# A selective-scan recurrence on one core: delta*u moved from GpSimd to VectorE, two products with C per batch moved the other way, softplus and the first inputs rearranged

## The chip, the core and the metric

The kernel runs on one core of one Trainium2 chip. The metric is the device time of one launch in microseconds (us). A profiled execution of the same program gives a trace: each instruction with its engine, its start, its duration and, where the engine stood idle ahead of it, what released it. The engines are TensorE (PE), VectorE (DVE), ScalarE (ACT), GpSimd (POOL) and SyncE (SP), which issues most DMAs. Each works through its own queue in order.

## What is computed

The whole program is a state-space layer, a mixture of experts with 64 experts, a cross attention and a quantised feed-forward layer over x of 4 x 512 x 512. The change lies in the first part alone. Cut to that, for each batch:

```python
x  = einsum('ed,bld->bel', in_proj_w, ctx)          # 512 channels, 512 steps
u  = silu(depthwise_conv(x, conv_w) + conv_b)
dt_lo, Bm, Cm = split(einsum('ke,bel->bkl', x_proj_w, u), [16, 16, 16])
delta = softplus(einsum('er,brl->bel', dt_proj_w, dt_lo) + dt_proj_b)
def step(state, d_t, B_t, C_t, u_t):                # state: channels x 16
    state = state * exp(d_t * A) + (d_t * u_t) * B_t
    return state, (state * C_t).sum(-1)
y = (scan(step) + D * u) * silu(layernorm(x_in))
x_out = x_in + y
```

## The kernel before

The channels lie on the 128 partitions in NC = 4 chunks c, and the 512 time steps in the free dimension. For a batch b (of 4) and a chunk c, the 16 states are taken two at a time, so that a pair of states is one tile of 128 x 1024. That makes 8 pairs i per chunk, 32 per batch, and a list `seq` of 128 steps q = (b, c, i) that one Python loop (L676) writes out. The loop's order of calls is the order of each engine's queue: the section runs under a manual schedule, and nothing reorders it. I call the eight steps of one (b, c) a **block**, and s = q % 32 the step within the batch.

What one step q does:

- `inputs(q + 2)` (L494), POOL: dBu = B (from `bb`, rows broadcast to all partitions) times du (delta*u), 128 x 1024, into one of three buffers. It runs two steps ahead; its buffer is that of step q - 1, which that step's scan must have read.
- `decays(q + 1)` (L502), ACT: two exponentials of delta into a dA tile in PSUM, of which there are two, so that step q - 1 must be done with its own. At s = 22 and s = 28 the decays of steps 24 and 30 are made early instead, in SBUF (`early=True`, L506).
- `scan(q)` (L513), DVE: the scan over dA and dBu (L524). Then the product with C (L525). For i in 0, 2 and 4 the scan writes to SBUF (`hc`) and POOL takes the product; for the others the scan writes in place over dA, and DVE takes the product.
- `sums(q - 1)` (L534), PE: eight transposes onto one PSUM tile `yT` sum the states; `result` (L562) multiplies the finished tile by the gate on DVE at i = 2 of the next block.

Once per block, for the block after: at i = 2 a matmul makes `pdt` in PSUM (L425); at i = 3 ACT runs `steps_a` and `steps_ln` (L428 to L443: e = |pdt|, relu = max(pdt, 0), e = exp(-e), pdt = 1 + e, ln); at i = 4 DVE runs the three instructions of `steps_b` (L450 to L452), which add max(pdt, 0) and ln(1 + e) with a correction; at i = 5 POOL makes du = delta*u (L460) and writes the reset value into delta's first column (L463). The tiles `pdt` lie in PSUM; `e`, `ln`, `delta`, `u` and `du` lie in SBUF.

Meanwhile the queues carry the next batch's projection, convolution and activations (`ahead`, `ahead_ends`), and the values and keys of the later attention on PE, ACT and SP. In `ahead`, at s = 26 `norm` (L384) makes 1/std on POOL with a power and -mean/std, at s = 29 `silu_gz` (L394) uses both on ACT, and at s = 26, 28 and 30 `rows` loads B and C by DMA.

Ahead of the loop (L648 to L674) the first batch is prepared: convolution, `tables` (an ACT table load, L242), project, softplus, `step_du`, and the inputs of steps 0 and 1.

Of the kernel before, what the change touches and what calls it, by code (L numbers as in the profile page):

```python
# [17 lines left out]
F32 = mybir.dt.float32  # L18
# [6 lines left out]
AF = mybir.ActivationFunctionType  # L25
ALU = mybir.AluOpType
# [4 lines left out]
P = 128  # L31
B, S, DM = 4, 512, 512
NT = B * S // P
NC = DM // P
CTX = 256
EPS = 1e-5
# [32 lines left out]
RESET = 1e30  # L69
# [172 lines left out]
def tables(nc):  # L242

    nc.scalar.preload_act_table_set("natural_log_exp_and_others")
# [3 lines left out]
def ssm_phase(ctx, cm, x_all, w, kv, router_stats):  # L248
# [4 lines left out]
    tc, nc = cm.tc, cm.nc  # L253
    pool = {n: ctx.enter_context(tc.tile_pool(name=f"a_p{n}", bufs=n)) for n in (1, 2, 3, 4, 5)}
# [15 lines left out]
    st = {}  # L270
# [17 lines left out]
    for n, shape in (("conv_w", [P, NC, DC]), ("conv_b", [P, NC]), ("D", [P, NC])):  # L288
        t = vecs[n] = cp.tile(shape, F32, name=f"v_{n}")
# [78 lines left out]

    def silu_0(c):
        nc.scalar.activation(st[0]["u"][c], st[0]["u"][c], AF.Silu)  # L370
        if c == NC - 1:
            tables(nc)

    def silu_u(b):
        for u in st[b]["u"]:
# [8 lines left out]
    def norm(b):  # L384
        s = st[b]
        ve = small.tile([P, NC], F32, name="ve_a")
        nc.gpsimd.tensor_scalar(ve, s["mv"][:, :, 1], EPS, None, ALU.add)
        s["rstd"] = small.tile([P, NC], F32, name="rstd_a")
        nc.gpsimd.tensor_tensor(s["rstd"], ve, half, ALU.pow)
        s["nmr"] = small.tile([P, NC], F32, name="nmr")  # L390
        nc.gpsimd.tensor_tensor(s["nmr"], s["mv"][:, :, 0], s["rstd"], ALU.mult)
        nc.gpsimd.tensor_scalar(s["nmr"], s["nmr"], -1.0, None, ALU.mult)

    def silu_gz(b):  # L394
        s = st[b]
# [7 lines left out]
    def project(b):  # L403
        pd = st[b]["pd"] = ps.tile([R, S], F32, name="pd", tag="pa")
        for c in range(NC):
            nc.tensor.matmul(pd, xpT[:, c, :], st[b]["u"][c], start=c == 0, stop=c == NC - 1)

    def take_project(b):

        xd = st[b]["xd"] = pool[1].tile([R, S], F32, name="xd")  # L410
        nc.scalar.activation(xd, st[b]["pd"], AF.Identity, bias=cm.ident[0:R, DR:DR + 1])
        nc.sync.dma_start(bc_dram[b], xd[R // 2:, :])

    def rows(b, g):

        for name, row in (("bb", g * NG), ("cb", DS + g * NG)):
            t = pool[4].tile([P, NG, S], F32, name=name, tag=name)
            nc.sync.dma_start(
                t, bc_dram[b, row:row + NG, :].unsqueeze(0).to_broadcast([P, NG, S]))
            st[b][name].append(t)  # L420
# [7 lines left out]
    def steps_a(b):  # L428

        s = st[b]  # L430
        pdt = s["pdt"]
        s["e"] = pool[1].tile([P, S], F32, name="e")
        s["relu"] = pool[2].tile([P, S], F32, name="delta")
        nc.scalar.activation(s["e"], pdt, AF.Abs)
        nc.scalar.activation(s["relu"], pdt, AF.Relu)
        nc.scalar.activation(s["e"], s["e"], AF.Exp, scale=-1.0)

    def steps_ln(b):

        s = st[b]  # L440
        nc.scalar.activation(s["pdt"], s["e"], AF.Identity, bias=cm.ones[:, 0:1])
        s["ln"] = pool[1].tile([P, S], F32, name="ln", tag="yg")
        nc.scalar.activation(s["ln"], s["pdt"], AF.Ln)  # L443

    def steps_b(b):


        s = st[b]
        t, delta = s.pop("pdt"), s.pop("relu")
        nc.vector.scalar_tensor_tensor(t, t, 1.0, s["e"], ALU.subtract, ALU.subtract)  # L450
        nc.vector.tensor_tensor(t, s["ln"], t, ALU.subtract)
        nc.vector.tensor_tensor(delta, delta, t, ALU.add)  # L452
        s["delta"].append(delta)

    def step_du(b):
        s = st[b]
        c = len(s["du"])
        delta = s["delta"][c]
        du = pool[2].tile([P, S], F32, name="du")
        nc.gpsimd.tensor_tensor(du, delta, s["u"][c], ALU.mult)  # L460


        nc.gpsimd.memset(delta[:, 0:1], RESET)  # L463
        s["du"].append(du)


# [17 lines left out]
    def take_values(b, n):  # L484
        g, kc = divmod(n, S // P)
        v = pool[2].tile([P, HG * HD], F32, name="v")
        nc.scalar.copy(v, pvs.pop((b, n)))
        nc.sync.dma_start(kv["v"][b, g, :, kc, :], v)
# [2 lines left out]
    seq = [(b, c, i) for b in range(B) for c in range(NC) for i in range(NP)]  # L491
    dBus, dAs, hcs, yTs = {}, {}, {}, {}

    def inputs(q):  # L494
        if q < len(seq):
            b, c, i = seq[q]
            j = i % 2 * 2
            dBus[q] = pool[3].tile([P, 2, S], F32, name="dBu")
            nc.gpsimd.tensor_tensor(dBus[q], st[b]["bb"][i // 2][:, j:j + 2, :],  # L499
                                    st[b]["du"][c].unsqueeze(1).to_broadcast([P, 2, S]), ALU.mult)  # L500

    def decays(q, early=False):  # L502

        if q < len(seq) and q not in dAs:
            b, c, i = seq[q]
            dAs[q] = (pool[2].tile([P, 2, S], F32, name="dA") if early else  # L506
                      pda.tile([P, 2, S], F32, name="dA"))
            for j in range(2):
                n = 2 * i + j
                nc.scalar.activation(dAs[q][:, j, :], st[b]["delta"][c], AF.Exp,  # L510
                                     scale=negA[:, c, n:n + 1])

    def scan(q):  # L513


        b, c, i = seq[q]
        j = i % 2 * 2
        cb = st[b]["cb"][i // 2][:, j:j + 2, :]
        hc = hcs[q] = pool[3].tile([P, 2, S], F32, name="hc")
        dA, dBu = dAs.pop(q), dBus.pop(q)  # L520
        on_pool = i in (0, 2, 4)
        h = hc if on_pool else dA
        flat = [t.rearrange("p a s -> p (a s)") for t in (h, dA, dBu)]
        nc.vector.tensor_tensor_scan(*flat, 0.0, ALU.mult, ALU.add)  # L524
        (nc.gpsimd if on_pool else nc.vector).tensor_tensor(hc, h, cb, ALU.mult)  # L525
# [20 lines left out]
    def direct(b, c):  # L546
        st[b]["Du"] = pool[1].tile([P, S], F32, name="Du")
        nc.scalar.activation(st[b]["Du"], st[b]["u"][c], AF.Copy, scale=vecs["D"][:, c:c + 1])
# [13 lines left out]
    def result(b, c):  # L562
        xv = x_all[:, b * NC:(b + 1) * NC, c * P:(c + 1) * P]
        if b + 1 < B:
            nc.vector.tensor_tensor(xv, yTs.pop((b, c)), st[b]["gzT"], ALU.mult)  # L565
            if c == NC - 1:
                nc.gpsimd.dma_start(x_all[:, b * NC:(b + 1) * NC, :],
                                    w["x"][b * S:(b + 1) * S, :].rearrange("(c p) d -> p c d", p=P),
                                    accum_op=ALU.add)
            return  # L570
        t = pool[1].tile([P, NC, P], F32, name="yg")
        nc.vector.tensor_tensor(t, yTs.pop((b, c)), st[b]["gzT"], ALU.mult)
        nc.gpsimd.tensor_tensor(xv, xv, t, ALU.add)
# [69 lines left out]
    def key_steps(q, ends):  # L643
        for f, a in key_plan.pop((q, ends), ()):
            f(*a)
# [11 lines left out]
    silu_0(3)  # L657
    project(0)
    take_project(0)
    rows(0, 0)  # L660
    for c in range(NC):
        stats(0, c)
# [5 lines left out]
    step_du(0)  # L668
    decays(0)
    decays(1)  # L670
    inputs(0)
    inputs(1)
    load_wv(0)
    for g in range(1, DS // NG):  # L674
        rows(0, g)
    for q, (b, c, i) in enumerate(seq):  # L676
        inputs(q + 2)

        ahead_of = b + 1 < B and q % 2 == 0 and q > 0
        if ahead_of:  # L680
            take_values(*last)
        decays(q + 1)
        key_steps(q, False)
        if b > 0 and q % SL == 1:
            rows(b, DS // NG - 1)
        if i == 2 and q > 2:
            result(*seq[q - 3][:2])
        scan(q)
        if i == 1:
            direct(b, c)  # L690
        if q == 0:
            silu_gz(0)
        if q % SL == 8 and b + 1 < B:
            load_x(b + 1)
        if i == 2:
            take_gate(b, c)

        to = seq[q // NP * NP + NP][0:2] if q + NP < len(seq) else None
        if to is not None:
            if i == 3:  # L700
                steps_a(to[0])
                steps_ln(to[0])
            if i == 5:
                step_du(to[0])
        if b + 1 < B:
            ahead(b + 1, q % SL)
        if i == 1:
            gate(b, c)
        if q % 8 == 2 and q + 8 < len(seq):
            load_wv(q // 2 + 4)  # L710
        if q % 2:
            values((b + 1) % B, q % SL // 2, wvs[q // 8])
        elif q > 0 and not ahead_of:
            take_values(*last)
        last = (b + 1) % B, q % SL // 2
        sums(q - 1)
        if to is not None:
            if i == 2:
                dt(*to)
            if i == 4:  # L720
                steps_b(to[0])
        if b + 1 < B:
            ahead_ends(b + 1, q % SL)
        key_steps(q, True)
# [1876 lines left out]
```

## Time and profile before

| what | value |
|---|---|
| median of 3 timed runs | 2467.73 us (2467.22 to 2468.25) |
| the profiled execution's own time | 2456.93 us |
| its span, first to last instruction | 2455.2 us |
| granted TensorE clock, mean | 0.982 |
| first scan starts, last scan starts | 34.46 us, 503.07 us |
| scans (L524) | 128 of 2300 or 2347 ns mean by form |
| products with C (L525) | 80 on DVE of 1256 ns, 48 on POOL of 2412 ns |
| inputs dBu (L499) | 128 on POOL of 2411 ns |
| delta*u (L460) | 16 on POOL of 1731 ns (1261 to 3277) |
| softplus on DVE (L450, L451, L452) | 16 each of 685, 696 and 686 ns |
| Relu on ACT (L435) | 16 of 596 ns |

The page's first part gives each engine's busy time; another view gives busy time by stretch; the timeline lists the instructions of one engine, with start, duration, engine, line, output<-inputs, shape and count, and in brackets the idle time ahead of them and what ended it. Two instructions of one engine may overlap by a tenth of a microsecond in it.

From the starts of the scans in the timeline, the time from the first scan of a block to the first scan of the next, in us:

| batch | c = 0 | c = 1 | c = 2 | c = 3 |
|---|---|---|---|---|
| 0 | 28.92 | 28.14 | 29.89 | 33.55 |
| 1 | 28.00 | 28.14 | 29.49 | 33.57 |
| 2 | 28.13 | 28.13 | 29.50 | 33.56 |
| 3 | 31.06 | 27.78 | 27.79 | 25.39 (to the last product) |

### The profile page before, as it was taken

The numbers are of one execution on the slowest core, as the hardware profiler recorded it, in microseconds if no ns is written. First come the engines' busy times: TensorE is split into PE (matmuls) and PEld (weight loads), VectorE is DVE, ScalarE is ACT, GpSimd is POOL, SyncE is SP. The second block draws the span as 40 slices with busy tenths as digits, with TensorE's granted clock in tenths as the row PEclk, the third lists the DMA queues.
The fourth block names the chain that finished last, engine by engine and source line by source line (L and its number), as shares of the span: only waits on it lengthen the run. The fifth ranks groups of instructions, "written<-read, shape, count | busy, mean of one in ns | idle before, by whom it ended". The sixth has DMA issues, their size and how long they took to land. (4 is left out here: it accounts for less than half of the span.)

```text
span 2455.2 us, 29177 instructions
## 1 busy us (share of the span) xinstructions
PE 2324.5 (95%) x8819; PEld 1264.5 (52%) x8819; DVE 1587.6 (65%) x2872; ACT 1413.3 (58%) x2647; POOL 1329.0 (54%) x1314
## 2 busy tenths in 40 slices
PE   6999899988999999999998899999999999999998
PEld 2555555655555656667674444444444444444444
DVE  6999998966244434444334577667776777666655
ACT  6777777755323333344433466666666676667654
POOL 7999999950444434544444356356644564333323
PEclk8999998999999999999999999999999999999999
DMA  5363727343789878899996488678867887676630
GB/s 214 91 230 95 237 88 247 112 152 122 213 262 289 266 227 275 274 284 341 297 275 205 147 197 208 152 183 208 191 149 168 181 200 170 137 155 148 135 75 26
DMA packets 479891, 468.01 MB, mean 191 GB/s; under 512 B 313247, under 2 KB 354287, under 8 KB 475632
## 3 DMA queue, kind: packets, MB, share of 16 engines
q1 hardware_dynamic: 433390, 303.41, 46.7%
q0 software_dynamic: 42992, 160.13, 20.7%
q10 hardware_dynamic: 3346, 2.54, 0.3%
q8 instruction: 72, 1.18, 0.2%
q14 instruction: 91, 0.75, 0.1%
HBM read 316.11 MB, written 79.82 MB: 161 GB/s over the span
## 5 line engine op out<-in xcount | busy, mean ns | idle before, releaser
L1350 PE MATMUL pg<-xT,wg 128*128 128x284 f32 (+12 forms) x1536 | 390.6, 400 | 3.5 <-ACT xT L1337 2.1
L2086 POOL COPY planes<-e 128x512 int16<-128x512 int16 x174 | 118.8, 683 | 397.6 <-DVE e L2067 227.7
L2058 DVE TENSOR_REDUCE mx<-psc 128x1 f32<-128x512 f32 x256 | 176.1, 688 | 239.7 <-PE psc L2055 239.0
L1350 PEld LDWEIGHTS pg<-xT,wg 128*128 128x128 f32 x1536 | 281.2, 192 | 94.4 <-issue 39.1
L499 POOL TENSOR_TENSOR dBu<-bb,du 128x1024 f32<-128x1024 f32 x128 | 304.7, 2411 | 6.1 <-DVE dA L524 5.3
L2061 ACT ACTIVATE e<-psc,mx 128x512 f32<-128x512 f32 x256 | 176.1, 688 | 152.6 <-DVE mx L2058 82.2
L2055 PE MATMUL psc<-kT,qT 128*128 128x512 f32 x512 | 260.1, 594 | 0.7 <-ACT qT L2049 0.7
L2127 PE MATMUL po<-eT,v 128*128 128x512 f32 x512 | 236.8, 605 | 13.7 <-ACT eT L2121 11.9
L1271 POOL DMA_INDIRECT xg<-xn_dram,tok x168 | 176.0, 1047 | 120.0 <-PE pt L1314 58.3
L2021 PE MATMUL pq<-Wq,xnT 128*128 128x512 f32 x512 | 232.1, 596 | 3.9 <-ACT xnT L1977 3.6
L2136 PE MATMUL px<-Wo,oT 128*128 128x512 f32 x512 | 231.2, 595 | 2.3 <-DVE qn L2039 2.3
L510 ACT ACTIVATE dA<-delta,negA 128x512 f32<-128x512 f32 x256 | 176.4, 694 | 53.0 <-DVE hc L525 38.6
L524 DVE TENSOR_TENSOR_SCAN dA<-dA,dBu 128x1024 f32<-128x1024 f32 x80 | 184.0, 2300 | 17.6 <-ACT dA L510 11.1
L1271 POOL DMA_INDIRECT wd<-down,widx x64 | 61.6, 962 | 228.7 <-PE po L1384 219.4
L2127 PEld LDWEIGHTS po<-eT,v 128*128 128x128 f32 x512 | 92.0, 189 | 151.1 <-issue 91.8
L2021 PEld LDWEIGHTS pq<-Wq,xnT 128*128 128x128 f32 x512 | 96.1, 191 | 127.6 <-issue 108.9
L2136 PEld LDWEIGHTS px<-Wo,oT 128*128 128x128 f32 x512 | 95.1, 190 | 125.4 <-issue 105.8
L530 PEld LDWEIGHTS yT<-ident,hc 128*128 128x128 f32 x1024 | 118.7, 143 | 73.4 <-issue 45.3
L1395 ACT COPY yo<-po 128x512 f32<-128x512 f32 (+3 forms) x64 | 37.4, 585 | 193.8 <-PE po L1384 147.7
L530 PE MATMUL yT<-ident,hc 128*128 128x128 f32 x1024 | 132.0, 276 | 16.6 <-DVE x_all L565 10.2
L1395 DVE COPY yo<-po 128x512 f32<-128x512 f32 x68 | 46.9, 690 | 150.2 <-PE po L1384 150.2
L2067 DVE TENSOR_SCALAR e<-e,tot 128x512 f32<-128x512 f32 x256 | 129.0, 504 | 13.5
(380 smaller groups left out, 4671.7 us busy)
## 6 DMA issues: line engine op xcount, KB each, us to landing
y_dram<-yo SPq DMA_DIRECT2D x110, 256.0 KB
bb<-bc_dram SPq DMA_DIRECT2D x16, 1024.0 KB
cb<-bc_dram SPq DMA_DIRECT2D x16, 1024.0 KB
v_dram<-v SPq DMA_DIRECT2D x64, 256.0 KB
kT<-k_dram SPq DMA_DIRECT2D x64, 256.0 KB
rk<-r_dram SPq DMA_DIRECT2D x64, 256.0 KB
v<-v_dram SPq DMA_DIRECT2D x64, 256.0 KB
Wo<-Wo SPq DMA_DIRECT2D x60, 256.0 KB
```

Source lines behind the costliest of these rows:

```text
L499: nc.gpsimd.tensor_tensor(dBus[q], st[b]["bb"][i // 2][:, j:j + 2, :], st[b]["du"][c].unsqueeze(1).to_broadcast([P, 2, S]), ALU.mult)
L510: nc.scalar.activation(dAs[q][:, j, :], st[b]["delta"][c], AF.Exp, scale=negA[:, c, n:n + 1])
L524: nc.vector.tensor_tensor_scan(*flat, 0.0, ALU.mult, ALU.add)
L530: nc.tensor.matmul(yT[:, lc, :], t[:, lc * P:(lc + 1) * P], cm.ident, is_transpose=True, start=first and lc == 0, stop=last, skip_group_ch ...
L1271: nc.gpsimd.indirect_dma_start(out=t[0:n, :], out_offset=None, in_=table, in_offset=bass.IndirectOffsetOnAxis(ap=index, axis=0))
L1350: nc.tensor.matmul(pg[:, 0:n], s["wg"][:, c, m * P:(m + 1) * P], s["xT"][:, c, 0:n], start=c == 0, stop=c == NC - 1)
L2021: nc.tensor.matmul(pq.rearrange("p h d -> p (h d)"), xnTs[b * NC + i][:, c, :], s["Wq"][:, c, :], start=c == 0, stop=c == NC - 1)
L2055: nc.tensor.matmul(pscore, st[b, g]["qT"][:, h, i * P:(i + 1) * P], ks[n], start=True, stop=True)
L2058: nc.vector.tensor_reduce(mx, pscore, AX.X, ALU.max, negate=True)
L2061: nc.scalar.activation(e, pscore, AF.Exp, bias=mx, accum_out=tot)
L2127: nc.tensor.matmul(po, v[:, kc, :], eT[:, kc, :], start=kc == 0, stop=kc == KB - 1)
L2136: nc.tensor.matmul(px, oTs[j * HG + h][:, i * P:(i + 1) * P], st[b, g]["Wo"][:, h, :], start=h == 0, stop=h == HG - 1)
```

## The change

1. `step_du`: the product delta*u and the write of the reset value go from POOL to DVE, and are called at i = 4 right behind `steps_b`, not at i = 5.
2. `scan`: the product with C of i = 6 goes from DVE to POOL for c = 1 and c = 2 of all batches but the last (six products); that of the very first step goes from POOL to DVE.
3. Softplus: ACT no longer makes the Relu; 1 + e goes to a tile `near` in SBUF (the later delta) and not over `pdt` in PSUM; the correction is worked out in that SBUF tile; the last DVE instruction reads `pdt` from PSUM, takes its maximum with 0 and adds.
4. `norm`: the addition of epsilon goes from POOL to DVE, and the two small instructions that make -mean/std become one on DVE. The power stays on POOL between them.
5. The inputs of step 0 are made by DVE.
6. At the start, the second ACT table load comes behind `take_project(0)`, not ahead of `project(0)`.

```diff
     def silu_0(c):
         nc.scalar.activation(st[0]["u"][c], st[0]["u"][c], AF.Silu)
-        if c == NC - 1:
-            tables(nc)
...
         ve = small.tile([P, NC], F32, name="ve_a")
-        nc.gpsimd.tensor_scalar(ve, s["mv"][:, :, 1], EPS, None, ALU.add)
+        nc.vector.tensor_scalar(ve, s["mv"][:, :, 1], EPS, None, ALU.add)
         s["rstd"] = small.tile([P, NC], F32, name="rstd_a")
         nc.gpsimd.tensor_tensor(s["rstd"], ve, half, ALU.pow)
         s["nmr"] = small.tile([P, NC], F32, name="nmr")
-        nc.gpsimd.tensor_tensor(s["nmr"], s["mv"][:, :, 0], s["rstd"], ALU.mult)
-        nc.gpsimd.tensor_scalar(s["nmr"], s["nmr"], -1.0, None, ALU.mult)
+        nc.vector.scalar_tensor_tensor(s["nmr"], s["mv"][:, :, 0], -1.0, s["rstd"], ALU.mult,
+                                       ALU.mult)
...
-        s["relu"] = pool[2].tile([P, S], F32, name="delta")
+        s["near"] = pool[2].tile([P, S], F32, name="delta")
         nc.scalar.activation(s["e"], pdt, AF.Abs)
-        nc.scalar.activation(s["relu"], pdt, AF.Relu)
         nc.scalar.activation(s["e"], s["e"], AF.Exp, scale=-1.0)
...
-        nc.scalar.activation(s["pdt"], s["e"], AF.Identity, bias=cm.ones[:, 0:1])
+        nc.scalar.activation(s["near"], s["e"], AF.Identity, bias=cm.ones[:, 0:1])
         s["ln"] = pool[1].tile([P, S], F32, name="ln", tag="yg")
-        nc.scalar.activation(s["ln"], s["pdt"], AF.Ln)
+        nc.scalar.activation(s["ln"], s["near"], AF.Ln)
...
-        t, delta = s.pop("pdt"), s.pop("relu")
-        nc.vector.scalar_tensor_tensor(t, t, 1.0, s["e"], ALU.subtract, ALU.subtract)
-        nc.vector.tensor_tensor(t, s["ln"], t, ALU.subtract)
-        nc.vector.tensor_tensor(delta, delta, t, ALU.add)
+        pdt, delta = s.pop("pdt"), s.pop("near")
+        nc.vector.scalar_tensor_tensor(delta, delta, 1.0, s["e"], ALU.subtract, ALU.subtract)
+        nc.vector.tensor_tensor(delta, s["ln"], delta, ALU.subtract)
+        nc.vector.scalar_tensor_tensor(delta, pdt, 0.0, delta, ALU.max, ALU.add)
...
-        nc.gpsimd.tensor_tensor(du, delta, s["u"][c], ALU.mult)
+        nc.vector.tensor_tensor(du, delta, s["u"][c], ALU.mult)
...
-        nc.gpsimd.memset(delta[:, 0:1], RESET)
+        nc.vector.memset(delta[:, 0:1], RESET)
...
-    def inputs(q):
+    def inputs(q, by=nc.gpsimd):
...
-            nc.gpsimd.tensor_tensor(dBus[q], st[b]["bb"][i // 2][:, j:j + 2, :],
+            by.tensor_tensor(dBus[q], st[b]["bb"][i // 2][:, j:j + 2, :],
                                     st[b]["du"][c].unsqueeze(1).to_broadcast([P, 2, S]), ALU.mult)
...
-        on_pool = i in (0, 2, 4)
+        on_pool = q > 0 and (i in (0, 2, 4) or i == 6 and c in (1, 2) and b + 1 < B)
...
     take_project(0)
+    tables(nc)
...
-    inputs(0)
+    inputs(0, nc.vector)
...
-            if i == 5:
-                step_du(to[0])
...
             if i == 4:
                 steps_b(to[0])
+                step_du(to[0])
```

## The prediction

> **What bounds the kernel now.** I read the page's first part, then busy time by stretch, then who waits for whom from 30 to 510 us, then the timelines of VectorE and GpSimd over batch 1. The first view is one batch of the recurrence:
>
> ```profile
> 155.00:275.00 120.00, 109.90 (x482) 64.89 (x483) 111.92 (x82) 89.18 (x146) 114.18 (x58) 0.96 0.50 163
> ```
>
> Of 120 us PE is busy 109.9, DVE 111.9, ACT 89.2 and POOL 114.2. So no single engine has room to take work for nothing, and only DVE's queue is in every step. DVE's waits, from 30 to 510 us (total, times, longest):
>
> ```profile
> DVE dA L524 <- ACT dA L510: 11.1, 9, 2.0
> DVE dA L524 <- POOL dBu L499: 4.5, 5, 1.6
> DVE pdt L450 <- ACT ln L443: 4.2, 3, 2.5
> DVE hc L524 <- POOL dBu L499: 3.9, 1, 3.9
> ```
>
> DVE stands for some 30 us out of 475 in all, and only 8.4 of them are put down to POOL, 3.9 of those at the start. The recurrence is therefore paced by DVE's own instructions. From the timeline's starts, a scan with POOL's product costs DVE 2.2 us, a scan with its own product 3.52, a result 0.6 and softplus this much:
>
> ```profile
> 167.79 2.28 DVE L524 TENSOR_TENSOR_SCAN hc<-dA,dBu 128x1024 f32<-128x1024 f32 x1
> 169.98 0.67 DVE L450 SCALAR_TENSOR_TENSOR pdt<-pdt,e 128x512 f32<-128x512 f32 x1
> 170.69 0.70 DVE L451 TENSOR_TENSOR pdt<-ln,pdt 128x512 f32<-128x512 f32 x1
> 171.42 0.69 DVE L452 TENSOR_TENSOR delta<-delta,pdt 128x512 f32<-128x512 f32 x1
> 172.03 2.29 DVE L524 TENSOR_TENSOR_SCAN dA<-dA,dBu 128x1024 f32<-128x1024 f32 x1
> ```
>
> The scan of i = 4 ends at 170.07 and the next starts at 172.03: 1.96 us. A block's floor is 3 x 2.2 + 5 x 3.52 + 0.6 + 2.05 = 26.85 us; blocks c = 0 to 2 take 28.0 to 29.9 with their statistics (0.81 each). What follows the recurrence needs all of its x, so I pass its time on one to one.
>
> **The row that decides.** Nearly every DVE instruction in the loop has one input in PSUM and at most one in SBUF. The exceptions are steps 24 and 30 of a batch, whose dA lies in SBUF. DVE, then POOL, around both in batch 1:
>
> ```profile
> 240.59 3.34 DVE L524 TENSOR_TENSOR_SCAN hc<-dA,dBu 128x1024 f32<-128x1024 f32 x1
> ...
> 264.32 2.69 DVE L524 TENSOR_TENSOR_SCAN dA<-dA,dBu 128x1024 f32<-128x1024 f32 x1
> 267.11 2.05 DVE L525 TENSOR_TENSOR hc<-dA,cb 128x1024 f32<-128x1024 f32 x1
> ```
>
> ```profile
> 239.43 2.37 POOL L499 TENSOR_TENSOR dBu<-bb,du 128x1024 f32<-128x1024 f32 x1 [1.11 <-DVE dA L524]
> ...
> 262.51 2.35 POOL L499 TENSOR_TENSOR dBu<-bb,du 128x1024 f32<-128x1024 f32 x1
> 264.83 3.26 POOL L460 TENSOR_TENSOR du<-delta,u 128x512 f32<-128x512 f32 x1
> 268.14 0.10 POOL L463 MEMSET delta<- 128x1 f32 x1
> 268.24 7.76 POOL L499 TENSOR_TENSOR dBu<-bb,du 128x1024 f32<-128x1024 f32 x3
> ```
>
> The scan of 3.34 is 1.06 over the usual 2.28: it works only from about 241.65, as POOL's dBu ends (241.80). The scan at 264.32 gains 0.4, to the end of POOL's dBu at 264.86. POOL's du, 1.28 at its median, then takes 3.26, as if begun at 266.8 when that scan ends. DVE's product at 267.11, 1.23 as a rule, ends at 269.16: begun at 267.93, as du ends. And POOL's three dBu, 6.99 elsewhere, take 0.77 more. So an instruction of DVE with two inputs in SBUF and one of POOL that reads SBUF take turns, each whole, and **the one that was waiting goes next**, even between two DVE instructions that follow on one another. The handover comes some 0.15 to 0.2 ahead of the recorded end. At 1410.59 a DVE instruction with two SBUF inputs (L1950, median 746 ns) takes 2.06 and ends 0.56 after POOL's product of 1410.82 to 1412.09. DMA does not explain it:
>
> ```profile
> 240.00:244.00 4.00, 4.00 (x22) 2.46 (x21) 4.00 (x3) 3.96 (x8) 1.79 (x1) 1.00 0.17 66
> 264.00:268.00 4.00, 4.00 (x16) 2.64 (x15) 3.90 (x3) 3.97 (x6) 4.00 (x2) 0.59 1.01 410
> ```
>
> The DMA engines are full in the second stretch but at 0.17 in the first, with the larger delay.
>
> The page "SBUF — State Buffer" of the Trainium skill, section "Who interferes with whom", says the same against this change: a VectorE instruction with two SBUF inputs and a GpSimd one that reads SBUF hold a shared port pair in turn, each for its whole length. Taken to the letter a turn costs 2.35 and not the 2.0 I use below; over two turns in each of 15 blocks that would be some 10 us more.
>
> **Part by part.**
> *Softplus and du (parts 1 and 3).* Today none of L450 to L452 has two SBUF inputs. After the change the first (near, e), the second (ln, near) and du (delta, u) do; the third reads PSUM. I take their lengths from L450 to L452, 0.65 to 0.7. POOL is free of du and waits at the product of i = 4 when that scan ends at T (its dBu was made before); DVE's first instruction starts at T - 0.09 and goes first, to T + 0.6. POOL's product then runs, 2.35, and holds the second one back by 2.0: T + 2.6 to 3.3. POOL's next dBu takes the turn (3.1 to 5.45), the third DVE instruction hides beside it, du waits to 5.3 and ends at 5.95. The scan of i = 5 starts at T + 5.95, today at T + 1.96: **+4.0 us a block**, du's own 0.65 included. The memset (0.06) is lost in it. Below, 2.0 a block if only one turn is lost; above, 6.2 if POOL is in mid-instruction at T and the first one waits a whole 2.2 as well.
> *Products to POOL (part 2).* DVE saves 3.52 - 2.2 = 1.32 in c = 1 and c = 2 of three batches; POOL, with time to spare now, hides 2.33.
> *Waits that go.* The small stalls at i = 2 and i = 6 come from PE and ACT running late, and those get time: I take 0.6 in c = 0, 0.3 in c = 1, 0.5 in c = 2. So c = 0: 4.0 - 0.6 = +3.4; c = 1: 4.0 - 1.32 - 0.3 = +2.4; c = 2: +2.2.
> *Norm (part 4), a new wait.* DVE's second instruction of s = 26 now needs POOL's power, which stands behind POOL's product of that step:
>
> ```profile
> 251.20 2.35 POOL L525 TENSOR_TENSOR hc<-hc,cb 128x1024 f32<-128x1024 f32 x1 [0.19 <-DVE hc L524]
> ...
> 253.96 1.04 POOL L389 TENSOR_TENSOR rstd_a<-ve_a,half 128x4 f32<-128x4 f32 x1
> ...
> 255.57 4.66 POOL L499 TENSOR_TENSOR dBu<-bb,du 128x1024 f32<-128x1024 f32 x2
> ```
>
> The scan of s = 26 ends at 251.06, the product at 253.55, the power about 1.05 later at 254.6. The next dBu starts at once and DVE's instruction, with two SBUF inputs, waits for it: ready at about 256.9. Queued behind it on DVE is the scan of s = 27, which starts at 250.97 today: 5.9 later (3.6 without the turn). Then 3.52, a scan of 2.2 and softplus at 5.95 put the scan of s = 29 at 268.6. Today it starts at 260.78 after 1.97 us of waiting for ACT; that wait, and the 1.45 at s = 31 behind `silu_gz`, are swallowed. Carried on (3.52, 1.0 for a turn at scan 30, then 3.5), s = 31 starts at 276.6 against 270.61: **+6.0 for c = 3**.
> *Last batch.* Its stall on ACT ln shrinks by the Relu's 0.48, but POOL's product is then already under way, so three full turns give T + 7.05; today the scan of i = 5 starts T + 4.68 (c = 0) and T + 2.95 (c = 1, c = 2): 2.4 + 4.1 + 4.1 = +10.6. Block c = 3 has no softplus.
> *Start (parts 5 and 6).* ACT's Relu (0.48) and POOL's du against DVE's (1.26 - 0.65) come off the way to the first decays: 1.1 to 1.5. The input by DVE may have to take turns with POOL's second input, 2.3 at worst, but scan 2 waits for ACT and the second B rows (37.6) anyway. I take -1.5. The moved table load gains 0.15.
>
> **Sum.** 3 x (3.4 + 2.4 + 2.2 + 6.0) + 10.6 - 1.5 = 42 + 10.6 - 1.5 = **+51, say 50 us**. The profiled execution's own time, 2456.93 with a span of 2455.2, would become 2507. The timed runs have a median 10.8 above it; with the same 50 they come to **2518 us**. Its own range is 2483 to 2552: below, one turn a block and no turn at norm (next paragraph, less 3 x 2.3); above, 15 x 2.2 more.
>
> **Rivals.** *One turn a block* (0.18): DVE keeps its place between dependent instructions, and only du waits: +2.0 a block, c = 0 to 2 then +1.4, +0.4, +0.2, c = 3 +4.0, last batch +6: 3 x 6 + 6 - 1.5 = +22, 2490. Against it stands the product at 267.11, which had to wait though it followed its scan.
> *No turns* (0.09): the long instructions have another cause. Then du costs 0.65, the products give 1.32 back, the norm wait of 3.6 goes into the waits of 1.97 and 1.45 behind it: about 3 x (0.65 - 0.7 - 0.7) + 0.6 - 1.5 = -3, 2465. The stretch at 240 speaks against it.
> *GpSimd paces the loop* (0.07), the faster case: POOL is the busiest, 114.2 of 120, and gives up 16 du and memsets (27.7 + 1.6), three small instructions a batch (2.6), one product and one input (4.7), and takes six products (14): -22.6, 2445. It decides if POOL never stands and DVE mostly waits for it; but only 8.4 of DVE's 30 us of waiting are for POOL.
>
> **Chances.** Forecast 0.66, one turn 0.18, no turns 0.09, GpSimd 0.07. About 0.2% (5 us) is what a measurement of this kernel can tell from no change: slower 0.84, within 0.09, faster 0.07. The range 2483 to 2552 leaves out the last two, 0.16.
>
> **What would show it.** In the new profile the second softplus instruction and du on DVE last 2 us and more, ending just after POOL's products or dBu, while the third stays at 0.7; the scan of i = 5 starts some 6 us after that of i = 4 ends; at s = 27 DVE idles 3.5 us for POOL's power; POOL's idle time grows and its busy share in the loop falls. If these three DVE instructions last 0.7, the turns were wrong and so is the forecast; if DVE's waits for POOL vanish with a shorter block, GpSimd was the pace.

## The result, and the profile after

| | before | after |
|---|---|---|
| median | 2467.47 us (2464.46 to 2468.25) | 2565.72 us (2555.62 to 2575.11) |
| profiled execution, its span | 2456.93, 2455.2 us | 2561.09, 2559.1 us |
| granted TensorE clock, mean | 0.982 | 0.961 |
| first scan starts | 34.46 us | 31.59 us |
| the last product with C ends | 506.7 us | 602.3 us |
| from there to the first matmul of the experts | 129.7 us | 138.1 us |
| the rest of the span | 1818.8 us | 1818.7 us |

The ratio is 1.041, 95% interval 1.0385 to 1.0436: slower, by twice what was forecast (2518), and outside the range. Of the span's 103.9 us, the recurrence brought 95.6 (forecast 51) and the stretch behind it 8.4 (forecast 0).

One batch of the recurrence, 120 us before, takes 147 now. Busy time by stretch (PE, PE's weight load, DVE, ACT, POOL, then clock, DMA share and GB/s):

```profile
177.00:324.00 147.00, 118.92 (x476) 69.92 (x476) 135.43 (x89) 87.45 (x140) 114.06 (x49) 0.88 0.40 132
```

POOL has as much busy time as before, in a longer batch: its share is 0.78, not 0.95. DVE is "busy" 135.4 of 147, and that is misleading: the time in which an instruction is held back is recorded as its own duration, not as idle time. The new code in the timeline of DVE, then of POOL, at i = 4 of c = 3 in batch 1 (start, duration):

```profile
302.02 2.28 DVE L521 TENSOR_TENSOR_SCAN hc<-dA,dBu 128x1024 f32<-128x1024 f32 x1
304.22 0.67 DVE L447 SCALAR_TENSOR_TENSOR delta<-delta,e 128x512 f32<-128x512 f32 x1
304.92 2.72 DVE L448 TENSOR_TENSOR delta<-ln,delta 128x512 f32<-128x512 f32 x1
307.68 0.69 DVE L449 SCALAR_TENSOR_TENSOR delta<-pdt,delta 128x512 f32<-128x512 f32 x1
308.41 2.00 DVE L457 TENSOR_TENSOR du<-delta,u 128x512 f32<-128x512 f32 x1
310.52 2.30 DVE L521 TENSOR_TENSOR_SCAN dA<-dA,dBu 128x1024 f32<-128x1024 f32 x1
```

```profile
304.38 2.71 POOL L522 TENSOR_TENSOR hc<-hc,cb 128x1024 f32<-128x1024 f32 x1 [1.12 <-DVE hc L521]
307.06 2.79 POOL L496 TENSOR_TENSOR dBu<-bb,du 128x1024 f32<-128x1024 f32 x1
```

That is the forecast's picture: four DVE instructions of one length (0.67 to 0.69 when nothing holds them). The first goes ahead of POOL; the second and du, with two inputs in SBUF as well, are held 2.0 and 1.3 us, to the end of POOL's product and of its dBu; the third, which reads PSUM, is not held. The scan of i = 5 starts 6.2 us after that of i = 4 ends; 5.95 was forecast. But this holds in two blocks of a batch, not in all. The steps that grew, from the starts of the scans in batch 1:

| | before | forecast | after |
|---|---|---|---|
| c = 0, i = 4 | 4.24 | 8.15 | 11.23 |
| c = 1, i = 4 | 4.69 | 8.15 | 10.46 |
| c = 2, i = 4 | 4.25 | 8.15 | 8.51 |
| c = 3, i = 4 | 6.29 | 8.15 | 8.50 |
| last batch, i = 4 (c = 0; 1 and 2) | 6.88; 5.16 | 9.25 | 11.84; 11.7 |
| c = 3, i = 2 (norm) | 2.19 | 8.1 | 9.81 |
| c = 3, i = 6 (dA in SBUF) | 6.29 | 4.5 | 6.77 |
| c = 0, i = 2; c = 2, i = 0; c = 2, i = 2 | 3.01; 3.00; 3.17 | less | 4.07; 4.67; 4.51 |

### The profile page after: what moved, and what is told of

Read it like the earlier page. It is cut to its first block, busy times and chain, and to the rows that moved or that the text cites. A ratio compares the mean times of both kernels' runs of the same rounds, so it can differ in the third digit from the quotient of the medians.

```text
span 2559.1 us, 29130 instructions
## 1 busy us (share of the span) xinstructions
PE 2367.9 (93%) x8819; PEld 1288.6 (50%) x8819; DVE 1678.5 (66%) x2908; ACT 1409.6 (55%) x2631; POOL 1323.0 (52%) x1274
## 3 DMA queue, kind: packets, MB, share of 16 engines
q10 hardware_dynamic: 3346, 2.54, 0.3%
## 5 line engine op out<-in xcount | busy, mean ns | idle before, releaser
L496 POOL TENSOR_TENSOR dBu<-bb,du 128x1024 f32<-128x1024 f32 x127 | 313.6, 2494 | 96.5 <-DVE dA L521 87.8
L2124 PE MATMUL po<-eT,v 128*128 128x512 f32 x512 | 236.8, 605 | 10.8 <-ACT eT L2118 9.1
L527 PE MATMUL yT<-ident,hc 128*128 128x128 f32 x1024 | 139.7, 286 | 68.1 <-DVE hc L522 61.2
L521 DVE TENSOR_TENSOR_SCAN dA<-dA,dBu 128x1024 f32<-128x1024 f32 x75 | 174.7, 2329 | 15.6 <-issue 10.3
L522 POOL TENSOR_TENSOR hc<-hc,cb 128x1024 f32<-128x1024 f32 x53 | 132.8, 2506 | 28.5 <-DVE hc L521 28.5
```

The costliest lines, as they stand in the source:

```text
L496: by.tensor_tensor(dBus[q], st[b]["bb"][i // 2][:, j:j + 2, :], st[b]["du"][c].unsqueeze(1).to_broadcast([P, 2, S]), ALU.mult)
L527: nc.tensor.matmul(yT[:, lc, :], t[:, lc * P:(lc + 1) * P], cm.ident, is_transpose=True, start=first and lc == 0, stop=last, skip_group_ch ...
L2124: nc.tensor.matmul(po, v[:, kc, :], eT[:, kc, :], start=kc == 0, stop=kc == KB - 1)
```

## The experiments

Each ratio is against runs of the kernel before on the same chip; the kernels ran on several chips, so compare the ratios and not the times. The part of the program behind the first matmul of the experts is the same in all of them, and still took from 1814 to 1835 us in the profiled executions; so where a difference is small I also give the end of the recurrence, which is 506.7 us before and 602.3 after. Four of the kernels make a ladder from before to after.

**The start alone (parts 5 and 6).** The kernel before, with `inputs(0, nc.vector)`, the first product on DVE and the moved table load.

> The kernel before with the start alone changed (parts 5 and 6: the first inputs and the first product on VectorE, the table load moved). First scan some 1 to 2 us earlier, the rest as before: 2465 to 2466 us, within 0.2%; if the second load of B rows or ACT sets the pace of the start, no change.

2459.32 us, ratio 0.9999 (0.9979 to 1.0018). No change; the recurrence ends at 507.4.

**The products as well (parts 2, 5 and 6).**

```diff
-        on_pool = i in (0, 2, 4)
+        on_pool = q > 0 and (i in (0, 2, 4) or i == 6 and c in (1, 2) and b + 1 < B)
```

> The kernel before with the six more products on GpSimd (part 2) and the start (parts 5 and 6) alone. GpSimd now has 29.4 us of work in the blocks c = 1 and c = 2 that take 28.1 and 29.5 today: theory, GpSimd becomes the pace there and eats the 1.32 that VectorE saves; -3 at the start, +0 to +3 later: 2465 to 2468 us. Rival, VectorE alone paces: 3 x 2.6 + 3 less: 2457.

2478.70 us, ratio 1.0076 (1.0049 to 1.0103): a miss, slower by some 19 us where next to no change was expected. The step of i = 6 does fall, from 4.35 to 3.00, in c = 1 and c = 2. But in c = 3 of batch 1 (38.81 us for 33.57) this is seen, in DVE's timeline and, below, in the busy time of a stretch just before (in the order given above):

```profile
268.56 2.30 DVE L522 TENSOR_TENSOR_SCAN dA<-dA,dBu 128x1024 f32<-128x1024 f32 x1 [3.12 <-ACT dA L508]
...
272.11 4.42 DVE L522 TENSOR_TENSOR_SCAN dA<-dA,dBu 128x1024 f32<-128x1024 f32 x1
```

```profile
261.00:265.00 4.00, 4.00 (x6) 1.69 (x5) 2.44 (x4) 2.19 (x4) 3.91 (x4) 0.50 0.99 395
```

PE had stood for a third of the 4 us from 253 (2.69 busy) and runs at half its clock here, ACT's decays come late and DVE waits 3.12 for them; the scan of s = 30, with both inputs in SBUF, takes 4.42 beside POOL. POOL, which here still has du to make, runs on in c = 3 without idling until 274 us: its backlog cost more than the products saved.

**And du on VectorE (parts 1, 2, 5 and 6).** The changed kernel with softplus and `norm` as before.

> The changed kernel with parts 3 and 4 undone (softplus and norm as before): what is left is delta*u on VectorE, the products, and the start. Theory, turns: du waits for one turn, step i = 4 is 5.3 to 6 against 4.25 before (15 times +1.2 = 18), the six products give back 8, the start 3: about 2473 us. Rival, more work on VectorE: 15 times 0.65 less 8 less 3: 2466. Rival, GpSimd paces: below 2455.

2497.42 us, ratio 1.0139 (1.0112 to 1.0165): missed, since it started from the products' loss and since du, its mean 2248 ns, often loses more than one turn.

**And softplus (all but part 4).**

```diff
-        nc.vector.tensor_scalar(ve, s["mv"][:, :, 1], EPS, None, ALU.add)
+        nc.gpsimd.tensor_scalar(ve, s["mv"][:, :, 1], EPS, None, ALU.add)
...
-        nc.vector.scalar_tensor_tensor(s["nmr"], s["mv"][:, :, 0], -1.0, s["rstd"], ALU.mult,
-                                       ALU.mult)
+        nc.gpsimd.tensor_tensor(s["nmr"], s["mv"][:, :, 0], s["rstd"], ALU.mult)
+        nc.gpsimd.tensor_scalar(s["nmr"], s["nmr"], -1.0, None, ALU.mult)
```

> The changed kernel with the small instructions of norm on GpSimd again (part 4 undone), all else changed. Theory: VectorE no longer waits for GpSimd's power and takes no turns there; the step i = 2 of the blocks c = 3 falls from 9.8 to 2.2 us, three times -7.6, of which the waits for ACT at s = 29 and s = 31 take back up to 5 in all: -18 to -23, about 2546 us. Rival, the wait hides behind PE and ACT, which are late there anyway: less than 5 us in all.

2547.50 us, ratio 1.0360 (1.0314 to 1.0405). That interval overlaps the whole's, 1.0385 to 1.0436; the recurrence ends 11.0 us earlier, at 591.3. The step of s = 26 falls from 9.8 to 4.6, but the next softplus step rises from 8.5 to 11.28, so the block gains 2.4 and not 7.6: DVE then waits 2.32 for POOL's dBu and 1.43 for ACT's ln, and its first softplus instruction takes a turn as well (1.93). Norm's wait stood mostly in place of others.

The ladder, as ratios and as ends of the recurrence in the profiled executions:

| parts | ratio | recurrence ends | step |
|---|---|---|---|
| none | 1 | 506.7 | |
| 5, 6 | 0.9999 | 507.4 | +0.7 |
| 2, 5, 6 | 1.0076 | 519.2 | +11.8 |
| 1, 2, 5, 6 | 1.0139 | 538.0 | +18.8 |
| 1, 2, 3, 5, 6 | 1.0360 | 591.3 | +53.3 |
| all | 1.0410 | 602.3 | +11.0 |

The steps hold for this order alone, and one of a few us can be chance: the recurrence of the run with parts 5 and 6 has single steps 1.7 us longer and 1.7 shorter than the kernel before has at the same place. The next four take one part out of the whole, or put one in by itself.

**Softplus undone.**

```diff
-        nc.scalar.activation(s["near"], s["e"], AF.Identity, bias=cm.ones[:, 0:1])
+        nc.scalar.activation(s["pdt"], s["e"], AF.Identity, bias=cm.ones[:, 0:1])
...
-        nc.vector.tensor_tensor(delta, s["ln"], delta, ALU.subtract)
+        nc.vector.tensor_tensor(t, s["ln"], t, ALU.subtract)
```

> The changed kernel with softplus as before (part 3 undone: Relu by ACT, the correction worked out in PSUM), all else changed. Theory, turns: the first two softplus instructions have at most one SBUF input again and last 0.7 us; only du still waits for a turn. The step i = 4 falls from 8.5 to 11.2 us to some 5.3 to 6 (about 7.5 in the last batch), 15 blocks make about -61, the stalls on PE and ACT give back a little more: about 2500 us. Rival, more work on VectorE: softplus is three VectorE instructions either way, so undoing part 3 only puts the Relu back on ACT; the time stays within 5 us of 2566. Rival, PE's granted clock as the cause of its own: step i = 4 stays above 8 us.

2511.85 us, ratio 1.0192 (1.016 to 1.0225). With the running value in PSUM the three instructions take 0.69 each again, du still loses turns (mean 1859 ns; 3.96 in c = 0 of batch 1), and the step of i = 4 there is 5.4 to 5.5 in c = 2 and c = 3. In c = 2 the step of i = 0 is back at 3.0.

**Softplus alone, on the kernel before.**

> The kernel before with part 3 alone: Relu gone from ScalarE, softplus' correction in SBUF, delta*u on GpSimd as before. Theory, turns: two VectorE instructions with two SBUF inputs a block, and GpSimd has its full load, so the first of them often waits for a whole instruction too: step i = 4 goes from 4.2 or 4.7 to 6.5 to 9, 15 times +2.3 to +4.5: +35 to +65, 2495 to 2525 us. Rival, more work on VectorE: no VectorE instruction is added, ScalarE saves 0.6 a block: 2450 to 2465.

2511.51 us, ratio 1.0219 (1.0191 to 1.0246), as on the ladder. Keeping softplus' running value of 128x512 in SBUF and not in PSUM is more than half of the loss, whether it is put in alone or taken out of the whole.

**du undone.**

> The changed kernel with delta*u and the reset value by GpSimd at i = 5 (part 1 undone), all else changed. Theory, turns: one of three turns goes, with 0.65 of VectorE's own work: step i = 4 falls by 2.0 in the blocks with a free GpSimd (8.5 to 6.5) and by 0.7 to 2 elsewhere, du by GpSimd costs little: -20 to -30, about 2540 us. Rival, more work on VectorE: only the 0.65 goes, 15 times: about 2556.

2526.29 us, ratio 1.0261 (1.0232 to 1.0289). That is 1.5%, some 37 us, below the whole: 2.5 us for each of the 15 blocks with a softplus, more than was expected.

**The products undone.**

```diff
-        on_pool = q > 0 and (i in (0, 2, 4) or i == 6 and c in (1, 2) and b + 1 < B)
+        on_pool = q > 0 and i in (0, 2, 4)
```

> The changed kernel with part 2 undone but for the first step: the six products with C of i = 6 are VectorE's again. Theory A (from the run of the products alone, which lost 0.76% where the prediction gave them 1.32 us each): the six products make GpSimd late for the next block, TensorE and ScalarE stand and c = 2 and c = 3 lose it. Undone, VectorE pays its 1.3 us six times, but the stalls at i = 0 and i = 2 of c = 2 go (4.67 and 4.51 us back to about 3.0 and 3.5) and the time falls by 5 to 20 us, to a ratio of 1.034 to 1.039 against the kernel before. Rival B (the prediction's term): with delta*u off GpSimd it has the time for them, they gain 1.32 x 6 = 8 us, and undoing them makes it slower: ratio 1.044 or more. Rival C: gain and loss cancel, 1.039 to 1.043.

2554.85 us, ratio 1.0395 (1.0369 to 1.0421). B, the prediction's term, falls; A and C are not told apart. In batch 1, c = 1 pays 1.37 more, and c = 2 and c = 3 get back 1.07 and 1.12 (c = 2, i = 0: 4.67 to 3.00; c = 3, i = 2: 9.81 to 8.01). A saving of 1.35 at one step was lost a few steps on, though not all of this is sure to come from the products: at i = 0 of c = 2 the runs with norm undone and with the epsilon addition back on POOL, which keep them, also have 3.2 to 3.6.

The last four kernels take the turns themselves apart.

**POOL only writes.** The changed kernel; POOL's product of i = 4 is left out, so that two of the sixteen states are missing from y, and three memsets of its tile stand in its place.

```diff
+        if i == 4:
+            for _ in range(3):
+                nc.gpsimd.memset(hc, 0.0)
+            return
```

> The changed kernel, but GpSimd's product of i = 4 is left out and three memsets of the same tile stand in its place, which write SBUF and read nothing (two of the sixteen states are missing from y). Theory, turns are for GpSimd's reads: in the blocks where GpSimd stands waiting at that point (c = 2, c = 3) the second softplus instruction runs beside the memsets at 0.7 instead of 2.7, du too while the memsets last; step i = 4 falls from 8.5 to about 5. Rival, any GpSimd instruction holds VectorE up: the second softplus instruction still ends just after a memset, 1 us or more, step i = 4 stays above 6.5.

2502.22 us, ratio 1.0169 (1.0134 to 1.0204); the recurrence ends at 543.8, 58.5 earlier. DVE, then POOL, at i = 4 of c = 3:

```profile
278.14 0.69 DVE L448 TENSOR_TENSOR delta<-ln,delta 128x512 f32<-128x512 f32 x1
...
279.59 0.69 DVE L457 TENSOR_TENSOR du<-delta,u 128x512 f32<-128x512 f32 x1
```

```profile
277.59 2.97 POOL L524 MEMSET hc<- 128x1024 f32 x3 [1.07 <-DVE hc L521]
```

POOL is at work from 277.59 to 280.56, the same tile is written, and both DVE instructions take 0.69: they wait for POOL's product, which reads SBUF, and not for its writes.

**The accumulating DMA elsewhere.** In the changed kernel POOL issues a DMA that adds x into `x_all` at i = 2 of c = 0; here it issues it at i = 6.

```diff
-            if c == NC - 1:
-                nc.gpsimd.dma_start(x_all[:, b * NC:(b + 1) * NC, :], ..., accum_op=ALU.add)
...
+        if q % SL == 6 and b > 0:
+            nc.gpsimd.dma_start(x_all[:, (b - 1) * NC:b * NC, :], ..., accum_op=ALU.add)
```

> The changed kernel with GpSimd's accumulating DMA onto x issued at step 6 of the next batch instead of step 2. In the blocks c = 0 of batches 1 to 3 the first softplus instruction lasted 6.6 us, through three GpSimd instructions on end, each of 2.85 instead of 2.36. Theory A, that DMA lengthens GpSimd's instructions and makes VectorE lose its turn: step i = 4 of these blocks falls from 11.2 to between 8.5 and 10.4, and the long GpSimd instructions move behind step 6; -3 to -8 us in all. Theory B, GpSimd simply has a backlog there: 11.2 stays.

2550.07 us, ratio 1.0372 (1.0337 to 1.0406), an interval that overlaps the whole's; the recurrence ends at 591.5, 10.8 earlier. First POOL and one line of DVE in the changed kernel, c = 0 of batch 1:

```profile
186.72 1.40 POOL L564 DMA_DIRECT2D x_all<-x  x1
...
189.94 5.20 POOL L496 TENSOR_TENSOR dBu<-bb,du 128x1024 f32<-128x1024 f32 x2
194.57 2.87 POOL L522 TENSOR_TENSOR hc<-hc,cb 128x1024 f32<-128x1024 f32 x1
196.89 2.85 POOL L496 TENSOR_TENSOR dBu<-bb,du 128x1024 f32<-128x1024 f32 x1
```

```profile
193.69 6.61 DVE L447 SCALAR_TENSOR_TENSOR delta<-delta,e 128x512 f32<-128x512 f32 x1
```

Behind the DMA, POOL's instructions are recorded with 2.85 to 2.9 us and overlap by half a microsecond; they start every 2.3 us as elsewhere, so POOL is not slower. DVE's instruction, ready at 193.69, is held through three of them, until the last ends, though two of the three are recorded as starting after it. In batch 0 the same place has no such DMA ahead of it: POOL has a backlog there too, without idle time from 44.27 to 57.21, and DVE gets its turn after each POOL instruction:

```profile
48.11 1.39 DVE L447 SCALAR_TENSOR_TENSOR delta<-delta,e 128x512 f32<-128x512 f32 x1
49.53 2.72 DVE L448 TENSOR_TENSOR delta<-ln,delta 128x512 f32<-128x512 f32 x1
```

With the DMA moved, in batch 2:

```profile
335.35 0.75 DVE L447 SCALAR_TENSOR_TENSOR delta<-delta,e 128x512 f32<-128x512 f32 x1
```

The step of i = 4 in c = 0 falls from 11.2 to 8.6 in batches 1 and 2, and by 1.1 in the last. The DMA's own 1.4 us on POOL's queue, now behind this place, is a part of that. In its new place one POOL instruction behind it is recorded with 2.54 us, then POOL idles and the next have 2.36 again.

**Only the epsilon addition back on POOL.**

```diff
-        nc.vector.tensor_scalar(ve, s["mv"][:, :, 1], EPS, None, ALU.add)
+        nc.gpsimd.tensor_scalar(ve, s["mv"][:, :, 1], EPS, None, ALU.add)
```

> The changed kernel with only norm's addition of epsilon on GpSimd again; the last instruction of norm stays on VectorE. In the changed kernel that addition, with one SBUF input, lasts 2.1 us on VectorE, to the end of GpSimd's pair of inputs. Theory: GpSimd is some 2 us behind at that point, and the power stands behind its product in any case; VectorE waits as long for the power and then for its turn: step i = 2 of the blocks c = 3 stays at 9.8 to 10.1, the time within 5 us of the changed kernel's. Rival: the turn of the addition is on the way: i = 2 falls to about 7.8, -6 us.

2567.25 us, ratio 1.0429 (1.0394 to 1.0464): no gain, as expected, since POOL's product, not the addition, holds the power back.

**TensorE kept busy.** Twenty transposes of zeros are added to each block's `yT`.

```diff
+            for _ in range(5):
+                for lc in range(NC):
+                    nc.tensor.matmul(yTs[b, c][:, lc, :], zero, cm.ident, is_transpose=True, ...)
```

> The changed kernel with 20 more transposes of a tile of zeros onto the sum of states after step i = 4 of each block, which fill TensorE's idle time while VectorE waits; they add nothing to y. Theory: TensorE's granted clock falls after that idle time (0.65 and 0.50 from 237 to 245 us, at the end of block c = 1 of batch 1), and its late work makes ScalarE's decays and then VectorE late at i = 0 and i = 2 of block c = 2 (4.7 and 4.5 us against 3.0 and 3.2 before). With the gap filled the clock stays higher there and these steps come down to 3.0 to 3.7: -5 to -15 us. Rival: TensorE is late because it has too much work there; 2.5 us more a block then make these steps longer, and the time grows by 5 to 20 us.

2566.01 us, ratio 1.0446 (1.0416 to 1.0476): inconclusive. In batch 1 the clock stays at 1.00 from 230 to 262 and the stalls of c = 2 shrink (3.0 at i = 0, 3.45 at i = 2). In batches 0 and 2 the step of i = 2 stays at 4.51, and that of i = 0 is 3.6, which the run with norm undone has without the filling. The recurrence ends at 594.6, 7.7 earlier, but the part behind the experts' first matmul takes 9.4 longer in this execution, and the total does not move.

## Why the prediction was right in kind and wrong in size

**The row that decides** was read rightly. Two SBUF inputs on DVE beside a POOL instruction that reads SBUF mean turns, and the rivals "one turn a block", "no turns" and "GpSimd paces the loop" fall with the lines at 302 us. Under the Trainium skill's page "SBUF — State Buffer", section "Who interferes with whom", a GpSimd instruction that only writes does not hold up such a VectorE instruction; the run with memsets agrees (0.69 us for 2.72 and 2.00). The same section says that the instruction issued first has the pair and the other waits for its whole length; the DVE instruction of 193.69 took 6.61 us, past POOL instructions recorded as starting after it, so for that place, as far as recorded starts tell the order, the measurement decides against it.

**The step that failed: "POOL is free of du and waits at the product of i = 4 when that scan ends at T (its dBu was made before)".** It holds in c = 2 and c = 3. In c = 1, POOL is in the middle of two dBu (224.79 to 229.47) when the scan ends at 227.49, and the first instruction takes 2.61 (DVE, then POOL):

```profile
227.41 2.61 DVE L447 SCALAR_TENSOR_TENSOR delta<-delta,e 128x512 f32<-128x512 f32 x1
...
224.79 4.68 POOL L496 TENSOR_TENSOR dBu<-bb,du 128x1024 f32<-128x1024 f32 x2
229.44 2.80 POOL L522 TENSOR_TENSOR hc<-hc,cb 128x1024 f32<-128x1024 f32 x1
```

So three turns are lost and not two; the prediction's upper bound, 6.2 a block, is the rule there (the step grew by 5.8). In c = 0 POOL is in mid-instruction as well, and in batches 1 to 3, behind the accumulating DMA, **"the one that was waiting goes next"** fails too. In the last batch the wait for ACT's ln was to shrink: it went from 2.5 to 2.3 us in c = 0, but from 0.8 to 1.9 and 1.8 in c = 1 and c = 2. Of the 44.6 us that were missing, c = 0 holds 10.7, c = 1 6.0, c = 2 11.0, c = 3 10.9 and the last batch 7.2; the start, 1.4 better than forecast, takes some back.

**"Waits that go" had the wrong sign.** The prediction gave the small stalls at i = 2 and i = 6 back to ACT and PE, -0.3 to -0.6 a block. They grew: +1.06 at i = 2 of c = 0, +1.67 and +1.34 at i = 0 and i = 2 of c = 2. While DVE is held, PE has nothing to sum; from 237 us on in the changed kernel:

```profile
237.00:241.00 4.00, 1.65 (x8) 1.65 (x9) 3.90 (x3) 1.38 (x2) 2.35 (x1) 0.65 0.00 0
241.00:245.00 4.00, 4.00 (x7) 1.80 (x6) 3.86 (x5) 1.38 (x2) 3.43 (x2) 0.50 0.00 0
```

```profile
248.40 0.58 ACT L484 COPY v<-pv 128x512 f32<-128x512 f32 x1 [5.46 <-PE pv L478]
```

PE is busy 1.65 of 4 us, then all 4 with only seven matmuls at half its clock; ACT, which copies PE's result between decays, waits 5.46 for it; and DVE's scan at 250.40 waits 1.59 for ACT. This chain of waits is shown. Whether the clock, and not the idle time alone, makes it so long stays open: one batch of the run with filled PE speaks for it, the others do not.

**Products to POOL (part 2):** the saving was right at its own step (1.35 for 1.32), but it was counted as -7.9 in all and is worth nothing or less: +11.8 on the ladder, where POOL still makes du, and undoing it in the whole, where it does not, loses nothing. POOL's "time to spare" is not at the place where the products go. "Only DVE's queue is in every step" had left out that POOL makes a dBu and ACT two decays in every step too, and that POOL was busy for 0.95 of a batch.

**Norm (part 4):** the wait is there (DVE, then POOL, in batch 1):

```profile
296.27 2.31 DVE L389 SCALAR_TENSOR_TENSOR nmr<-mv,rstd_a 128x4 f32<-128x4 f32 x1 [3.28 <-POOL rstd_a L387]
...
292.91 2.35 POOL L522 TENSOR_TENSOR hc<-hc,cb 128x1024 f32<-128x1024 f32 x1
295.20 1.03 POOL L387 TENSOR_TENSOR rstd_a<-ve_a,half 128x4 f32<-128x4 f32 x1
```

DVE waits 3.28 for the power and then loses a turn, 9.8 us scan to scan for 8.1, since POOL came to the product 1.9 us after its scan had ended. With the products undone the step is 8.01. The "1.0 for a turn at scan 30" was 3.2: scan and product both lost a turn (3.34 and 3.40 for 2.28 and 1.23). The block, forecast at +6.0 with its softplus, grew by 9.6. Norm's own part of it is smaller than its wait: undone, only 2.4 a batch came back, because POOL's and ACT's lateness stood behind it. What DVE waits for, and what POOL does, from 30 to 640 us:

```profile
POOL dBu L496 <- DVE dA L521: 87.8, 36, 5.2
...
DVE nmr L389 <- POOL rstd_a L387: 9.9, 3, 3.3
...
DVE delta L447 <- ACT ln L440: 6.0, 3, 2.3
```

POOL now stands 87.8 us waiting for DVE's scans (5.3 before, from 30 to 510 us), as forecast: the work that it lost did not buy anything.

**"I pass its time on one to one"** missed 8.4 us. The stretch from the last product to the first expert matmul, before and after:

```profile
506.70:636.40 129.70, 108.09 (x604) 68.17 (x602) 70.53 (x251) 72.70 (x141) 33.37 (x93) 0.93 0.41 138
```

```profile
602.30:740.40 138.10, 119.25 (x610) 73.15 (x608) 70.59 (x251) 72.70 (x141) 33.49 (x93) 0.85 0.39 131
```

DVE, ACT and POOL have the same work to within 0.12 us; PE has nearly the same count and 11 us more, at a clock of 0.85 for 0.93. In the twelve other runs it takes 131.6 to 140.2 us at a clock between 0.93 and 0.87. The shortest has the highest of these clocks and the longest the lowest, but between them the order fails (133.6 us at 0.88, 137.7 at 0.90). What makes this stretch longer, and why the clock is lower there, was not settled.

**Start:** 2.9 us came off the first scan for 1.5. Parts 5 and 6 by themselves brought 0.8 of that (first scan at 33.63), and lost 1.2 again at the first step (3.47 for 2.30).

## What to carry to other kernels

Before an elementwise operation is put beside a busy GpSimd, count its inputs in SBUF: with two, its price is up to a whole GpSimd instruction on top of its own length, and one operand kept in PSUM avoids it (0.69 us for 2.72). Take GpSimd to be in mid-instruction, the upper bound, unless the timeline shows its queue standing at that very point, and do not count on stalls elsewhere to shrink: an engine that is held makes others late (here TensorE, then ScalarE, then VectorE again). DVE's busy time and a freed engine's spare share say nothing on this; equal instructions with unequal durations do.

## What the runs showed of the hardware that was not expected

- Behind the accumulating DMA on POOL's queue, its next instructions were recorded with 2.85 us for 2.35 and overlapped, and a DVE instruction with two SBUF inputs was held through three of them (6.61 us). With the DMA moved it took 0.75; with the same backlog and no DMA (batch 0), 1.39.
- An instruction of one small SBUF input takes part as well: DVE's addition of epsilon on 128 x 4 elements took 2.09 us (from 290.89), to the end of POOL's dBu pair (292.96). In the Trainium skill's "SBUF — State Buffer", section "Who interferes with whom", `tensor_scalar` is among the operations that can take both port pairs; this trace agrees.
- The granted clock of TensorE was 0.65 and then 0.50 (237 to 241, 241 to 245 us) after a stretch in which it was mostly idle (1.92 of 4 us busy from 233, 1.65 from 237), and four matmuls of the convolution then took 3.62 us instead of 1.88.
